# A 64-image chain of four convolution and scan layers on one core: the last norm's scale spread by a matmul in setup, and another order of the opening's convolution jobs

## The chip, the cores and the metric

The kernel runs on one NeuronCore of a Trainium2 chip. The metric is the device time in microseconds (us) from start to end of one launch; lower is better. Several launches are timed and the median is taken; one further launch is recorded by the hardware profiler. The engines are called PE (TensorE), DVE (VectorE), ACT (ScalarE), POOL (GpSimd) and SP (SyncE, which here only issues transfers).

## The reference, cut to what matters

The input is 64 images of 96 channels, 28 x 28, float32. Each passes through four layers, each with its residual:

- Layer 0: 1x1 expansion from 96 to 576 channels, norm, SiLU; a depthwise 5x5 convolution whose kernel is mixed per image from four experts; norm, SiLU; squeeze-and-excite; a 1x1 projection to 96 channels whose weights are also mixed from four experts; the last norm (`bn3`); add the input.
- Layers 1 and 3: expansion, norm, ReLU; depthwise 3x3, norm, ReLU; projection, the last norm, add the input.
- Layer 2: the image is cut in four quarters. On each: group norm, two 1x1 projections, a depthwise 3x3, and a selective scan (16 states, four directions), then group norm, a gate and a channel attention.

The last norm is `y * (g / sqrt(v + eps)) + ...` per output channel, so its factor can be multiplied into the projection's weights once, before any image:

```
inv = gamma * rsqrt(var + eps)
return (x - mean) * inv + beta
```

## The kernel before, in words

**Setup** (`Kernel.setup`, before L555) loads the weights in packed blobs, turns every norm into a scale and a bias (`bn`, L522, with `rsqrt`, L515: an add on DVE, then a power of -1/2 on POOL), multiplies `bn3`'s scale into the projection weights (`fold_bn3`, L535), expands the depthwise taps of layers 1 and 3 to diagonal blocks (`spread_taps`, L544, on POOL) and stores them and the four scaled experts of layer 0 to DRAM (`taps`, `w3_0`). Output channels lie along the free axis of the projection weights, so `fold_bn3` needs the scale as a row that is the same on all 128 lanes. Before the change this row is computed on all lanes: `bn3gr` and `bn3vr` are packed as 128 equal rows of 96, and the power runs over 128 x 96. That happens once for each of the four experts and once each for layers 1 and 3. Setup's scratch tiles come from a pool `fold` (two buffers per name) that is released when setup ends; the work tiles of the main part reuse its memory.

**The main part** keeps four images in flight. A *job* is one convolution layer on one image: `expand` (ten matmuls into PSUM, ACT applies norm and activation into padded tiles `border` and `hborder`, ACT's queue stores them to DRAM scratch `ex`), then per *unit* of channels `load` (SP loads shifted rows `rep`, and taps `wd`, from DRAM; for layer 0 POOL builds `wd` from the mixed kernel `kern`) and `depthwise` (20 matmuls a unit in layer 0, 12 a half-unit in layers 1 and 3, ACT evicts to `acc`), then `project` (18 or 10 matmuls, DVE adds to the image). Layer 0 has 9 units, layers 1 and 3 have 5 each; layer 0 also has `routing` and, ahead of its projection, `squeeze_excite`, which mixes the stored experts to `wp`. A `job(layer, t, ex)` names its layer, its image and its scratch.

Layer 2 on an image is two *halves*. `head` does norms, projections and the step sizes `dd`; `scans` then runs 12 groups of three DVE instructions per half (a product `b`, a scan `h`, a reversed scan `g`; before L1307, L1312, L1317), POOL combines them to `yc` (L1267), PE sums into `y` (L1241), and `tail` ends the half (last instruction L1396).

A *slot* runs layer 2 on image t beside the jobs of layer 1 on t+1, layer 0 on t+2 and layer 3 on t-1. There are 64 slots: slot 0 after an *opening*, 7 loop iterations of 8, then 7. The opening brings image 0 through layers 0 and 1 and image 1 through layer 0, and expands layer 1 of image 1 ahead.

The order on each engine is set by `Plan`: every operation has a due time, buffers and an estimated cost; `run` places operations greedily and chains each engine's instructions in that order, not earlier than 45 units before due. Buffers of one pool are taken in the order in which the operations were created (save `ps` and `gs`), so the order in which the jobs are written down also binds `rep` (3 buffers), `wd` (3) and `expert` (3). The hardware then runs each engine's list in order, waiting on semaphores only. Opening and slot 0 are one such plan, each loop iteration another; at the seam each engine goes on as soon as its own list is done.

Of the kernel before, what the change touches and what calls it, by code (L numbers as in the profile page):

```python
# [9 lines left out]
F32 = mybir.dt.float32  # L10
AF = mybir.ActivationFunctionType
ALU = mybir.AluOpType
AX = mybir.AxisListType
PSUM = bass.MemoryType.PSUM

P = 128
C = 96
# [4 lines left out]
E = 4  # L22
RH = 24
NS = 16
R = 6
# [6 lines left out]
NG = 9  # L32
# [42 lines left out]
def _rows(v):  # L75
    return np.tile(np.asarray(v)[None, :], (P, 1))
# [39 lines left out]
def pack_l0(ins):  # L116
    q = {k[len("L0_conv_") :]: np.asarray(v) for k, v in ins.items() if k.startswith("L0_conv_")}
    p = Pack()
    p.add("r_w1", q["r_w1"].T)
    p.add("r_b1", q["r_b1"][:, None])  # L120
    p.add("r_w2", q["r_w2"].T)
    p.add("r_b2", _rows(q["r_b2"]))
    p.add("w1", q["exp_w"].T)
    _pack_bn(p, "bn1", q, "bn1_g", "bn1_b", "bn1_m", "bn1_v", _lanes)
    _pack_bn(p, "bn2", q, "bn2_g", "bn2_b", "bn2_m", "bn2_v", lambda a: _groups(a, 16))

    dw = np.zeros((96 + RH, E, 360), np.float32)
    for e in range(E):
        dw[:96, e] = _taps(q["dw_w"][e].reshape(HID, 5, 5), 16).reshape(96, 360)
    dw.reshape(96 + RH, E * 360)[96:, : NG * P] = _groups(q["se_w2"], 16).transpose(2, 1, 0).reshape(RH, NG * P)  # L130
    p.add("dw", dw)
    p.add("mask", _pairs(np.repeat(np.eye(16, dtype=np.float32), 6, axis=0), 16))
    p.add("parity", _parity(16))
    p.add("se_w1", _groups(q["se_w1"].T, 16))
    b1 = np.zeros((96 + RH, 1), np.float32)
    b1[96:, 0] = q["se_b1"]
    p.add("se_b1", b1)
    p.add("se_b2", _groups(q["se_b2"], 16))
    p.add("bn3gr", _rows(q["bn3_g"]), once=True)
    p.add("bn3vr", _rows(q["bn3_v"]), once=True)  # L140
    _pack_bn(p, "bn3", q, "bn3_g", "bn3_b", "bn3_m", "bn3_v", None)
    return p

# [7 lines left out]
def pack_l1(ins, layer):  # L151
    pre = f"L{layer}_conv_"
    q = {k[len(pre) :]: np.asarray(v) for k, v in ins.items() if k.startswith(pre)}
    p = Pack()
    p.add("w1", q["w1"][:, :, 0, 0].T)
    _pack_bn(p, "bn1", q, "g1", "b1", "m1", "v1", _lanes)
    p.add("dw", _taps(q["wd"].reshape(HID, 3, 3), 32).reshape(P, 18 * 6), once=True)
    p.add("mask", _pairs(np.repeat(np.eye(32, dtype=np.float32), 4, axis=0), 32), once=True)
    _pack_bn(p, "bn2", q, "g2", "b2", "m2", "v2", _lanes)
    p.add("w3", _lanes(q["w3"][:, :, 0, 0].T))  # L160
    p.add("bn3gr", _rows(q["g3"]), once=True)
    p.add("bn3vr", _rows(q["v3"]), once=True)
    _pack_bn(p, "bn3", q, "g3", "b3", "m3", "v3", None)
    return p

# [280 lines left out]
class Kernel:  # L446
# [8 lines left out]
        g=(3, [P, 4, LSEQ]),  # L455
        yc=(3, [P, 4, SEQ]),
        B=(2, [P, 2, HALF]),
        C=(2, [P, 2, HALF]),
        dd=(4, [P, 3, HALF]),
        tmp=(2, [C, HALF]),  # L460
        gs=(3, [C, 32]),
        expert=(3, [P, 5 * C]),
# [7 lines left out]
        ps=(5, [P, 512]),  # L470
# [3 lines left out]
    def __init__(self, ctx, tc, x, out, blobs, packs):  # L474
        self.tc, self.nc = tc, tc.nc
        nc = tc.nc
# [12 lines left out]
        with self.tc.tile_pool(name="fold", bufs=2) as fold:  # L489
            engines = (nc.sync, nc.scalar, nc.sync, nc.scalar)  # L490
            self.c = []
            for i, (blob, p) in enumerate(zip(blobs, packs)):
                keep = self.tile([P, p.keep], f"blob{i}")
                once = fold.tile([P, blob.shape[1] - p.keep], F32, name=f"once{i}", bufs=1)
                engines[i].dma_start(keep, blob[:, : p.keep])
                engines[i].dma_start(once, blob[:, p.keep :])
                self.c.append(Consts(keep, once, p.at))
            self.setup(fold)
        self.slots = {name: n for name, (n, _) in self.POOLS.items()}
        work, psum = pool("work", 1), pool("psum", 1, space=PSUM)  # L500
        self.pools = {name: psum if name in ("ps", "y") else work for name in self.POOLS}
# [30 lines left out]
        nc.vector.tensor_tensor(bias, b, bias, ALU.subtract)  # L532
        return scale, bias

    def fold_bn3(self, c, w3, eps):  # L535

        nc = self.nc
        inv, tmp = self.inv
        self.rsqrt(inv, c("bn3vr"), eps, tmp)
        nc.vector.tensor_tensor(inv, inv, c("bn3gr"), ALU.mult)  # L540
        k = w3.shape[1]
        nc.vector.tensor_tensor(w3, w3, inv.rearrange("p (a o) -> p a o", a=1).to_broadcast([P, k, C]), ALU.mult)

    def spread_taps(self, out, taps, mask):  # L544

# [6 lines left out]
            ALU.mult,  # L552
        )

    def setup(self, fold):  # L555
        nc = self.nc
        c0, c1, c2, c3 = self.c
        self.eps, self.half1 = self.tile([C, 1], "eps"), self.tile([C, 1], "half1")
        nc.vector.memset(self.eps, 1e-5)
        nc.vector.memset(self.half1, 0.5)  # L560
        self.mhalf = self.tile([P, C], "mhalf")
        nc.vector.memset(self.mhalf, -0.5)

        self.inv = tuple(fold.tile([P, C], F32, name=f"inv{i}", bufs=1) for i in range(2))

        self.bn1_0 = self.bn(c0, "bn1", 1e-3, "l0")
        self.bn2_0 = self.bn(c0, "bn2", 1e-3, "l0")
        _, self.b3_0 = self.bn(c0, "bn3", 1e-3, "l0")
        for e in range(E):
            t = fold.tile([P, NG, C], F32, name="expert")  # L570
            nc.sync.dma_start(t.rearrange("p g o -> p (g o)"), self.experts[e])
            self.fold_bn3(c0, t, 1e-3)
            nc.sync.dma_start(self.w3_0[e], t.rearrange("p g o -> p (g o)"))

        self.ir = {}
        for layer, c in ((1, c1), (3, c3)):
            k = f"l{layer}"
            bn1 = self.bn(c, "bn1", 1e-5, k)
            bn2 = self.bn(c, "bn2", 1e-5, k)
            _, b3 = self.bn(c, "bn3", 1e-5, k)  # L580
            self.fold_bn3(c, c("w3"), 1e-5)
            self.ir[layer] = dict(c=c, bn1=bn1, bn2=bn2, b3=b3)

            for u in range(5):
# [5 lines left out]
                nc.sync.dma_start(self.taps[layer][u][:, : 32 * n], t[:, : 32 * n])  # L590


        with self.tc.tile_pool(name="fold_ps", bufs=1, space=PSUM) as banks:

            self.wdelta = self.tile([C + 1, C], "wdelta")
            ps = banks.tile([P, 512], F32, name="fold_ps0")
            nc.tensor.matmul(ps[:C, :C], c2("xdt"), c2("wdt")[:R], start=True, stop=True)
            nc.vector.tensor_copy(self.wdelta[:C], ps[:C, :C])
            nc.vector.tensor_copy(self.wdelta[C:], c2("wdt")[C:])
            ps = banks.tile([P, 512], F32, name="fold_ps")  # L600
            nc.tensor.matmul(ps[:C, :1], c2("p1"), c2("ln_b"), start=True, stop=True)
            nc.vector.tensor_tensor(c2("p1_b"), c2("p1_b"), ps[:C, :1], ALU.add)
            ps = banks.tile([P, 512], F32, name="fold_ps2")
            nc.tensor.matmul(ps[C : C + 1, :C], c2("ln_b"), c2("p2")[:C], start=True, stop=True)
            nc.vector.tensor_tensor(c2("p2")[C:], c2("p2")[C:], ps[C : C + 1, :C], ALU.add)
            for name in ("p1", "p2"):
                nc.vector.tensor_scalar(c2(name)[:C], c2(name)[:C], c2("ln_g"), None, ALU.mult)
        self.A = self.tile([P, NQ * J], "A")
        nc.scalar.activation(self.A, c2("A"), AF.Exp)
        nc.vector.tensor_scalar(self.A, self.A, -1.0, None, ALU.mult)  # L610
# [28 lines left out]
        self.ex = {(i, k): self.dpool.tile([HID, 2, 16, 32], F32, name=f"ex{i}_{k}") for i in range(3) for k in (3, 5)}  # L639
        for t in self.ex.values():  # L640
            nc.sync.dma_start(t[4 * P :].rearrange("c o r w -> c (o r w)"), self.pads[0][:64].rearrange("c o r w -> c (o r w)"))
        self.npad = self.ndecay = 0


# [781 lines left out]
            self.tail(q)  # L1426
        yield

    def slot(self, i, t, load, store, expanded=True, last=0):

        nc, pl, base, span = self.nc, self.plan, i * self.T, self.T
        keys = lambda t: [("x", t % 4, h) for h in range(2)]
        m = self.mamba(t, base, span, last < 2)
        next(m)
        jobs = []
        if last < 2:
# [16 lines left out]
        for _ in m:  # L1455
            pass

    def block(self):
        self.plan = Plan(self)
        return self.plan  # L1460
# [3 lines left out]
def mk_conv_seq_kernel(ctx, tc, x, out, blobs, packs):  # L1464
# [1 line left out]
    n = k.x.shape[0]  # L1466
    at = lambda v, i: v[bass.ds(i, 1)].rearrange("n c l -> (n c) l")
    pl = k.block()
    k.convs(
        -150.0, 150.0, [(k.job(0, 0, 1), None), (k.job(0, 1, 2), None), (k.job(1, 0, 1), None)], ahead=k.job(1, 1, 0)  # L1470
    )
    pl.due = -20.0
    k.head(k.half(0, 0))
    k.slot(0, 0, None, None)
    pl.run(-150.0)
    with tc.For_i(0, (n - 4) // 8, 1) as it:  # L1476
        pl = k.block()
# [34 lines left out]
```

## Time and profile before

| what | us |
|---|---|
| runs timed | 10371.73, 10323.82, 10363.91 |
| median | 10363.91 |
| the profiled execution's own time | 10374.65 |
| its span | 10372.8 |
| first routing instruction of the opening (L894) starts | 142.45 |
| first scan product (L1307) of slot 0 starts | 368.17 |
| last gate of slot 0 (L1396) starts | 524.84 |
| first scan product of the loop's first slot starts | 539.68 |

In the profile a line number L is that of the kernel's source; "x6" counts instructions; "idle before <- X" is time an engine had nothing to run, and X is what ended it. A float32 matmul shows as two records, so a layer-0 unit is 40 records of L786. "PEclk" is the share of full TensorE clock that was granted. Over the whole span PE is busy 9300.0 us (90%), DVE 8658.4 (83%), POOL 7409.3 (71%), ACT 6556.1 (63%), but these are averages over stages with different limits; setup, opening and slot 0 are 540 us of 10373.

### The profile page before, as it was taken

To read this page: it belongs to the slowest core of one execution; us is meant where nothing else is said; L and a number is where in the kernel's file an instruction comes from. 1 tells how busy PE (TensorE), PEld (TensorE's weight loads), DVE (VectorE), ACT (ScalarE), POOL (GpSimd) and SP (SyncE) were. 2 spreads that over 40 slices of the span, in tenths; PEclk is the share of its full clock that TensorE was granted. 3 is DMA by queue.
4 is the path that set the end of the run, shared out by engine and by line. 5 is a ranking of instruction groups with operands and counts; after the bars stand their busy time and mean duration, and the time that the engine had idled before them with its cause. 6 is when DMAs were issued, how large, how long until landed. Compare 5 with 4: busy or idle time off the path is not lost. (4 is left out here: it accounts for less than half of the span.)

```text
span 10372.8 us, 197146 instructions
## 1 busy us (share of the span) xinstructions
PE 9300.0 (90%) x75526; PEld 3900.2 (38%) x75526; DVE 8658.4 (83%) x8711; ACT 6556.1 (63%) x10733; POOL 7409.3 (71%) x7523
## 2 busy tenths in 40 slices
PE   4789998899989999899998999989999899998995
PEld 1333333334333433334333333333333333333342
DVE  1588897889878888788897899878897898888897
ACT  1466666666666666666665666666766666766663
POOL 5477776777767777677776777767776777767776
PEclk9889999999999999999999999989999999999997
DMA  4488887888878888788887888788887888877884
GB/s 140 136 225 222 233 239 214 222 226 238 235 213 220 225 235 231 201 225 226 231 240 204 224 240 235 214 218 220 228 242 211 223 231 219 230 218 212 231 237 114
DMA packets 1132620, 2262.68 MB, mean 218 GB/s; under 512 B 105984, under 2 KB 891136, under 8 KB 1131520
## 3 DMA queue, kind: packets, MB, share of 16 engines
q1 hardware_dynamic: 877120, 1750.78, 65.4%
q10 hardware_dynamic: 254528, 498.91, 13.7%
q8 instruction: 613, 10.04, 0.4%
q14 instruction: 359, 2.94, 0.1%
HBM read 1725.77 MB, written 523.50 MB: 217 GB/s over the span
## 5 line engine op out<-in xcount | busy, mean ns | idle before, releaser
L786 PE MATMUL ps<-rep,wd 128*32 128x392 f32 (+1 forms) x50688 | 4860.3, 522 | 383.5 <-DMA rep<-ex 93.9
L1312 DVE TENSOR_TENSOR_SCAN h<-decay,b 128x788 f32<-128x788 f32 x1536 | 2751.4, 1791 | 386.3 <-POOL g L1267 151.9
L786 PEld LDWEIGHTS ps<-rep,wd 128*32 128x32 f32 (+1 forms) x50688 | 1657.2, 112 | 3056.9 <-issue 2415.4
L1317 DVE TENSOR_TENSOR_SCAN g<-decay,b 128x788 f32<-128x788 f32 x1536 | 2727.4, 1776 | 28.8 <-DVE b L1307 3.2
L1267 POOL TENSOR_TENSOR yc<-h,g 128x392 f32<-128x392 f32 x1536 | 1576.1, 1045 | 1120.6 <-DVE b L1307 654.5
L797 ACT ACTIVATE acc<-ps,l_bn2b,l_bn2s 128x392 f32<-128x392 f32 x1728 | 1158.0, 674 | 1736.7 <-PE ps L786 1443.4
L1267 POOL TENSOR_TENSOR yc<-yc,C 128x392 f32<-128x392 f32 x1536 | 1565.0, 1037 | 456.8 <-DVE b L1307 385.3
L1307 DVE TENSOR_TENSOR b<-dd,B 128x784 f32<-128x784 f32 x1536 | 1816.3, 1182 | 43.1 <-issue 2.5
L1289 ACT ACTIVATE decay<-dd,A 128x784 f32<-128x784 f32 x1536 | 1364.3, 942 | 718.1 <-DMA dd<-ddd 422.6
L1267 POOL TENSOR_TENSOR g<-h,g 128x392 f32<-128x392 f32 x1536 | 1558.7, 1035 | 309.6 <-DVE b L1307 297.6
L1267 POOL TENSOR_TENSOR yc<-yc,g 128x392 f32<-128x392 f32 x1536 | 1433.6, 952 | 145.7 <-DVE b L1307 145.7
L684 PE MATMUL ps<-x,blob 96*128 96x392 f32 x3072 | 1296.7, 558 | 121.6 <-PEq L1476 33.6
L668 ACT ACTIVATE border<-ps,l_bn1b,l_bn1s 128x392 f32<-128x392 f32 x1536 | 986.8, 675 | 395.1 <-PE ps L684 277.3
L548 POOL TENSOR_TENSOR wd<-kern,blob 96x640 f32<-96x640 f32 x576 | 765.4, 1335 | 301.8 <-PE ps L786 173.7
L684 PEld LDWEIGHTS ps<-x,blob 96*128 96x128 f32 x3072 | 581.2, 206 | 780.1 <-issue 286.2
L855 PE MATMUL ps<-acc,blob 128*96 128x392 f32 (+1 forms) x2560 | 826.9, 505 | 29.2 <-ACT acc L797 13.0
L855 PE MATMUL ps<-acc,wp 128*96 128x392 f32 x2304 | 781.1, 497 | 34.7 <-DVE wp L995 34.3
L1289 ACT ACT_TABLE_LOAD x422 | 541.4, 1283 | 73.0 <-ACT border L668 37.5
L855 PEld LDWEIGHTS ps<-acc,wp 128*96 128x96 f32 x2304 | 371.6, 164 | 437.8 <-issue 380.9
L1241 PE MATMUL y<-yc,blob 128*32 128x392 f32 x3072 | 450.6, 524 | 86.7 <-POOL yc L1267 86.6
L855 PEld LDWEIGHTS ps<-acc,blob 128*96 128x96 f32 (+1 forms) x2560 | 352.7, 162 | 461.7 <-issue 361.7
L1082 POOL TENSOR_TENSOR gs<-gs,mhalf 96x2 f32<-96x2 f32 x256 | 188.7, 737 | 449.0 <-ACT gs L1079 273.9
(145 smaller groups left out, 7448.9 us busy)
## 6 DMA issues: line engine op xcount, KB each, us to landing
rep<-ex SPq DMA_DIRECT2D x1024, 448.0 KB, 7.5
rep<-ex SPq DMA_DIRECT2D x1984, 224.0 KB, 5.1
ex<-border ACTq DMA_DIRECT2D x512, 480.0 KB, 5.7
dd<-ddd SPq DMA_DIRECT2D x384, 588.0 KB, 6.8
wd<-taps SPq DMA_DIRECT2D x512, 384.0 KB, 6.7
ex<-border ACTq DMA_DIRECT2D x256, 512.0 KB, 5.6
B<-bcd SPq DMA_DIRECT2D x256, 392.0 KB, 4.1
C<-bcd SPq DMA_DIRECT2D x256, 392.0 KB, 5.2
```

The lines of the kernel that those rows point to most:

```text
L548: self.nc.gpsimd.tensor_tensor(out, taps.rearrange("k (n a) -> k n a", a=1).to_broadcast([k, n, cb]), mask.rearrange("k (a c) -> k a c", a ...
L668: nc.scalar.activation(dst, ps()[:, :HALF].rearrange("p (r o w) -> p o r w", o=2, w=28), d["func"], bias=bias[:, t : t + 1], scale=scale[: ...
L684: nc.tensor.matmul(ps()[:, :HALF], w1[:, t * P : t * P + P], x[:, h * HALF : (h + 1) * HALF], start=True, stop=True)
L786: nc.tensor.matmul(ps()[lo : lo + 32, :HALF], w, rep()[: (k + 1) * cb, b, :, 2 - off + dx : 30 - off + dx], start=(dx == 0), stop=(dx == k ...
L797: nc.scalar.activation(acc()[lo : lo + n], ps()[lo : lo + n, :HALF], d["func"], bias=bias[lo : lo + n, at : at + 1], scale=scale[lo : lo + ...
L855: nc.tensor.matmul(banks[o]()[:C, :HALF], w, a, start=(i == 0), stop=(i == (8 if d["layer"] == 0 else 4)))
L1241: nc.tensor.matmul(y()[32 * j : 32 * j + 32, :HALF], c("sel"), ys[j]()[:, 2 * u : 2 * u + 2], start=(k == 0 and u == 0), stop=(k == 1 and ...
L1267: nc.gpsimd.tensor_tensor(*vs, op)
L1289: nc.scalar.activation(fs[:, :, u, :, :SEQ], d()[:, :2].rearrange("p o (i l) -> p o i l", i=2), AF.Exp, scale=self.A[:, at : at + 1],)
L1307: nc.vector.tensor_tensor(out, v, w, ALU.mult)
L1312: lambda h=h, ff=ff: nc.vector.tensor_tensor_scan(flat(h()), ff, b, 0.0, ALU.mult, ALU.add),
L1317: lambda g=g, ff=ff: nc.vector.tensor_tensor_scan(flat(g())[:, ::-1], ff[:, ::-1], b[:, ::-1], 0.0, ALU.mult, ALU.add),
```

## The change

Two things are changed; loop and final slots keep, instruction for instruction, the order they had on every engine.

Setup: `bn` already makes `bn3`'s scale as a column (one channel per lane, 96 x 1). `row_of` multiplies an identity matrix by this column on DVE and multiplies a matrix of ones by the result on PE, which gives the row on all 128 lanes in PSUM; `fold_bn3` reads it from there. The row is made once for layer 0 and once each for layers 1 and 3. The packed rows `bn3gr` and `bn3vr` go, an identity `eye` comes, and `mhalf` shrinks from 96 columns to 9. The four experts get four buffers and are all loaded early; their scaling on DVE and their stores move to setup's end. The PSUM pool `fold_ps` now spans all of setup.

Opening: `opening` replaces a call of `convs` and writes down the jobs in another order, and slot 0's layer 2 gets due times 45 units earlier (`lead`).

```diff
-    p.add("bn3gr", _rows(q["bn3_g"]), once=True)
-    p.add("bn3vr", _rows(q["bn3_v"]), once=True)
+    p.add("eye", np.eye(C, dtype=np.float32), once=True)
...
-    def fold_bn3(self, c, w3, eps):
+    def row_of(self, banks, scale, eye, name):
         nc = self.nc
-        inv, tmp = self.inv
-        self.rsqrt(inv, c("bn3vr"), eps, tmp)
-        nc.vector.tensor_tensor(inv, inv, c("bn3gr"), ALU.mult)
+        nc.vector.tensor_scalar(eye[1], eye[0], scale, None, ALU.mult)
+        ps = banks.tile([P, 512], F32, name=name)
+        nc.tensor.matmul(ps[:, :C], self.ones[:C], eye[1], start=True, stop=True)
+        return ps[:, :C]
+
+    def fold_bn3(self, row, w3):
         k = w3.shape[1]
-        nc.vector.tensor_tensor(w3, w3, inv.rearrange("p (a o) -> p a o", a=1).to_broadcast([P, k, C]), ALU.mult)
+        self.nc.vector.tensor_tensor(w3, w3, row.rearrange("p (a o) -> p a o", a=1).to_broadcast([P, k, C]), ALU.mult)
...
-        self.mhalf = self.tile([P, C], "mhalf")
+        self.mhalf = self.tile([P, NG], "mhalf")
...
-        _, self.b3_0 = self.bn(c0, "bn3", 1e-3, "l0")
-        for e in range(E):
-            t = fold.tile([P, NG, C], F32, name="expert")
+        s3, self.b3_0 = self.bn(c0, "bn3", 1e-3, "l0")
+        eye = c0("eye"), fold.tile([C, C], F32, name="diagonal", bufs=2)
+        row = self.row_of(banks, s3, eye, "fold_row0")
+        experts = [fold.tile([P, NG, C], F32, name="expert", bufs=E) for e in range(E)]
+        for e, t in enumerate(experts):
             nc.sync.dma_start(t.rearrange("p g o -> p (g o)"), self.experts[e])
-            self.fold_bn3(c0, t, 1e-3)
-            nc.sync.dma_start(self.w3_0[e], t.rearrange("p g o -> p (g o)"))
...
-            _, b3 = self.bn(c, "bn3", 1e-5, k)
-            self.fold_bn3(c, c("w3"), 1e-5)
+            s3, b3 = self.bn(c, "bn3", 1e-5, k)
+            self.fold_bn3(self.row_of(banks, s3, eye, f"fold_row{layer}"), c("w3"))
...
+        for e, t in enumerate(experts):
+            self.fold_bn3(row, t)
+            nc.sync.dma_start(self.w3_0[e], t.rearrange("p g o -> p (g o)"))
         self.npad = self.ndecay = 0
...
-        m = self.mamba(t, base, span, last < 2)
+        m = self.mamba(t, base - lead, span, last < 2)
...
+    def opening(self):
+        pl = self.plan
+        first, second, other, ahead = self.job(0, 0, 1), self.job(1, 0, 1), self.job(0, 1, 2), self.job(1, 1, 0)
...
+        def units(d, us, due, each):
+            for i, u in enumerate(us):
+                pl.due = due + each * i - 14.0
+                self.load(d, u)
+                pl.due = due + each * i
+                self.depthwise(d, u)
...
+        expand(first, -150.0)
+        self.routing(first)
+        units(first, range(4), -150.0, 5.0)
+        expand(other, -140.0)
+        self.routing(other)
+        units(first, range(4, NG), -130.0, 5.0)
+        project(first, -105.0)
+        units(other, range(5), -103.0, 5.0)
+        expand(second, -85.0)
+        units(second, range(5), -68.0, 4.0)
+        project(second, -48.0)
+        pl.due = -46.0
+        self.head(self.half(0, 0))
+        units(other, range(5, NG), -44.0, 5.0)
+        project(other, -24.0)
+        expand(ahead, -18.0)
...
-    k.convs(
-        -150.0, 150.0, [(k.job(0, 0, 1), None), (k.job(0, 1, 2), None), (k.job(1, 0, 1), None)], ahead=k.job(1, 1, 0)
-    )
-    pl.due = -20.0
-    k.head(k.half(0, 0))
-    k.slot(0, 0, None, None)
+    k.opening()
+    k.slot(0, 0, None, None, lead=45.0)
     pl.run(-150.0)
```

## The prediction

> **What bounds it now.** The page's 90% PE is an average; the change touches only the first 540 us. So I first read busy time by stretch (columns: stretch, length, busy us of PE, PE's weight load, DVE, ACT and POOL, granted TensorE clock, DMA share, GB/s):
>
> ```profile
> 0.00:50.00 50.00, 5.46 (x14) 2.35 (x14) 13.67 (x53) 3.46 (x4) 38.43 (x23) 1.00 0.41 135
> 50.00:100.00 50.00, 0.48 (x1) 0.00 (x0) 7.37 (x11) 0.00 (x0) 47.60 (x7) 1.00 0.16 55
> 100.00:150.00 50.00, 5.12 (x12) 2.46 (x13) 10.34 (x14) 2.21 (x5) 36.77 (x7) 1.00 0.30 92
> 150.00:200.00 50.00, 45.97 (x350) 19.00 (x352) 7.11 (x23) 22.01 (x40) 13.06 (x10) 1.00 0.82 225
> ...
> 400.00:450.00 50.00, 9.93 (x26) 2.48 (x26) 48.52 (x36) 11.02 (x17) 39.93 (x44) 0.57 0.16 49
> ```
>
> Setup, to 142 us, is POOL alone. From 150 PE is full. In slot 0 DVE is full (48.52 of 50) and PE nearly empty. The groups of the first 150 us say what POOL does:
>
> ```profile
> L520 POOL TENSOR_TENSOR inv<-inv,mhalf 128x96 f32<-128x96 f32 x6 | 94.0, 15669 | 5.9 <-DVE expert L542 5.0 <-DVE blob L542 0.9
> L548 POOL TENSOR_TENSOR taps<-once 128x768 f32<-128x768 f32 x8 | 11.8, 1477 | 4.3 <-DMA once<-w_dram 4.3
> L540 DVE TENSOR_TENSOR inv<-inv,once 128x96 f32<-128x96 f32 x6 | 7.9, 1314 | 92.8 <-POOL inv L520 92.8
> ```
>
> Six powers of 15.67 us fill it, and DVE waits for them (92.8). The timeline shows what releases the opening, then DVE's way through slot 0:
>
> ```profile
> 142.45 2.72 DVE L894 TENSOR_REDUCE rw<-x 96x1 f32<-96x784 f32 x3 [3.83 <-DMA taps<-taps]
> ...
> 368.17 1.62 DVE L1307 TENSOR_TENSOR b<-dd,B 128x784 f32<-128x784 f32 x1 [2.16 <-DMA dd<-ddd]
> ...
> 494.76 1.77 DVE L1317 TENSOR_TENSOR_SCAN g<-decay,b 128x788 f32<-128x788 f32 x1
> ...
> 524.84 0.75 DVE L1396 SCALAR_TENSOR_TENSOR x<-ps,cz,x 96x196 f32<-96x196 f32 x2 [4.80 <-ACT cz L1390]
> ...
> 539.68 0.97 DVE L1307 TENSOR_TENSOR b<-dd,B 128x784 f32<-128x784 f32 x1
> ```
>
> L894 waits for setup's last transfers, since its tile takes over the memory of `fold`. Layer 2 of image 0 runs 368.17 to 496.5; the loop's first product follows at 539.68. That last mark is my yardstick: the rest of the program has the same order before and after, so its 9833 us (10372.8 - 539.7) should stay.
>
> **What the Trainium skill says.** *GPSIMD Engine Reference*, section 3.1, gives a two-input operation some 2.6 cycles an element; the trace's power is far dearer, 0.545 us on 96x1 and 15.67 on 128x96, 0.16 us a column, so the trace decides. [...]the trace has 2.4 at the median. *TensorE: Matmul & The Clock Gate*, Part 1, says that an idle array falls to half clock; the trace agrees, with 0.50 granted from 420 to 440 where PE is busy 4.28 of 20 us.
>
> **Part 1, the row.** Removed: 6 x 15.67 = 94.0 us of POOL, plus six L540 and L519 on DVE. Added, three times: a DVE product of 96x96 (the like of L607, 0.27), a matmul (L597, 0.63 for its two records) and the clearing of `ones` (0.14 for 128x96). These 3 us lie beside POOL, which still works through its taps; without that cover they would cost their 3 us. The product with the experts reads PSUM now; 1.05 became at most 1.3 by the like of L885, beside POOL too.
>
> What is late next? POOL keeps 27 us of work. Small powers start at 16.06; layer 0's take 3.45, layers 1 and 3 take 2.8 each, one tap 1.47, the clearing of borders 2.25: POOL stands at 28.8 with two of ten taps built. The other eight share two buffers, and each third build waits until a store has landed: 1.48 + 2.4 = 3.9 us a pair, 15.6 for four pairs, so 44.5. On SP six halo stores of 256 KB stand between the taps' stores; I add 1. SP then issues the four expert stores, moved behind the taps: 1.77 MB at 300 GB/s (early slices of the transfer rows reach 301 to 394) is 5.9, plus 2 for landing: 54 to 55. The built order has the opening's first reduce (L899 after) wait for these stores. Their data is ready: the loads go out at 12 to 13 us and land in 5.5 at the median, DVE's four products are done by some 34. So setup ends near **55 instead of 142.45: -87**. Bounds: 48 if stores don't hinder each other (-94); 68 if a tap's store takes 5 us, as a busy DMA did with `rep<-ex` (5.1) (-74).
>
> At the opening's start ACT waited 3.6 us for halo stores (L668 <- DMA ex<-border). They are issued before the expert stores now: **-3** (0 to -4).
>
> **Part 2, the opening,** in times of before. PE's stretch of first and second image read:
>
> ```profile
> 230.14 12.09 PE L855 MATMUL ps<-acc,wp 128*96 128x392 f32 x36
> 242.16 3.56 PE L786 MATMUL ps<-rep,wd 96*32 96x392 f32 x40
> ...
> 266.51 10.26 PE L786 MATMUL ps<-rep,wd 128*32 128x392 f32 x96 [0.89 <-DMA wd<-taps]
> ```
>
> A layer-0 unit is 3.4 us, a layer-1 half-unit 2.2, a layer-0 projection 12.1, an expansion 6.65. In the new order PE does 14 units, not 15, before the first projection: image 0 is ready at 239. Expansion to 246. Now nothing covers its way through DRAM: `rep` buffers go in the order written, so the other image's last four units queue behind. First store issued near 241.5, landing 5.7, the first `rep` (448 KB) 7.5 more: PE restarts near 255, **9 us idle**. Nine half-units (19.8), the projection (6.5), eviction and add end at 283, where before image 0 was ready at 325.4. From there to the first scan product took 42.8 (325.4 to 368.17). The chain is the same; ACT has fewer evictions but a gate's table load (1.28) in it. I take 327 for 368.17: scans start **41 earlier**.
>
> Is that kept? Twenty-four groups at 4.8 us (405.89 to 439.64 is seven) and some 12 of other DVE work end at 454; before they ended at 496.5. But PE, DVE and ACT have not finished their lists. By the built order POOL makes four of the nine `wd` of slot 0's layer-0 job only after its last `yc`, PE therefore has four units after the last `y`, then squeeze-and-excite, then projection, and DVE has the expert mixing and both image adds *behind* layer 2's last gate and ahead of the loop. Working it out: last `y` at 462, four units 14 to 23 (474.68 shows 5.7 for one at low clock), gate and sums near 480 to 485, mixing 15 (483.77 to 498.75 before, its expert loads one by one), rest of the projection 9, second add at 510. Expansion 6.7, then the loop's own 14.6 to its routing result (L1396 524.84 to L912 539.1): first product of the loop at 532 to 533. **So of 41 only 7 stay.** Before, this job ran beside the scans. Bounds: +12 if mixing waits for its loads longer (the opening's took 35 from sums to add, 207 to 242), -41 if PE's clock stays full and the tail hides.
>
> SP's list: `dd` loads stand behind four expert loads that need mixing; by my times they are issued five us before `dd` is stored, cost nothing, and would push the scans by what they are late.
>
> **Sum:** -87 - 3 - 7 = **-97 us**. Against the profiled execution, 10374.65 (span plus 1.85), that is 10278. That execution lay 10.7 above the median 10363.91; against the median it is **10267**. The runs shown spread 48 us.
>
> **The rivals.**
> *The whole lead arrives.* PE's idle 40 of 50 us in slot 0 speaks for it, POOL's order of `wd` against it. -87 - 3 - 41: 10233.
> *The tail costs more than the lead brings*, by 12 to 20 us: 10364 - 90 + 15 = 10289; for it, the 35 us from sums to add; against it, fewer transfers then (103 GB/s at 480 to 500).
> *Setup is held by transfers, so the power's removal brings only half.* 14.09 MB move before 150 us; at the 135 GB/s of the first 50 us they would need 104. Then setup gains 38, and the sum is -48: 10316. Against it: those slices with work reach 300.
> *Slower, by place of tiles.* `mhalf` shrinks from 384 to 36 bytes a lane, and every later constant and work tile lies 320 bytes lower. Should that slow DVE, POOL or the transfers, it does so in 63 slots of 156.1 us (9833 / 63). From 97 / 63 = 1.54 us a slot, 1%, the gain is gone; 2.4 us a slot makes 10418. Nothing in the trace shows a dependence on place; nothing excludes it.
>
> **The numbers.** About 0.5%, 52 us, is what a measurement of this kernel can tell from no change: faster means below 10312. The forecast 0.60, the whole lead 0.17, costly tail 0.13, held setup 0.07, slower 0.03. The first three are faster: 0.90; the fourth same, 0.07. The range reaches from the whole lead with setup at its fast bound (-94 - 4 - 41: 10225) and 5 us below it for the spread of runs, 10220, to the costly tail by 20 with setup at its slow bound and nothing at the opening's start (-74 + 20: 10310), 10312 with the same thought rounded to the edge of no change.
>
> **What would show it.** Right: no POOL instruction over 2 us before 60; L899 near 55, released by an expert store; PE idle some 9 us ahead of layer 1's first units; the first scan product 131 earlier (near 237), the loop's first only 97 earlier (near 443), with L872 ahead of it. Wrong: L899 after 75, the loop's first product before 415 or after 470, or a span from there to the end other than 9833 by over 25.

## The result, and the profile after

The changed kernel takes **10250.44 us**, the median of four runs (10225.01 to 10259.11), against 10360.36 for the kernel before in the same series: a ratio of 0.9896, 95% interval 0.9866 to 0.9926. In a second series of its own (experiment e4) it is 0.9883, 0.9865 to 0.9902. The forecast was 10267: the direction was right, and the median is 17 us below the forecast. The profiled execution took 10225.01 us, its span is 10223.2: the fastest of its four, which matters below.

I read the same views as for the kernel before. First, busy time by stretch (stretch, length, busy us of PE, PE's weight load, DVE, ACT, POOL, granted TensorE clock, DMA share, GB/s), of the kernel after:

```profile
0.00:50.00 50.00, 8.10 (x20) 3.88 (x20) 22.96 (x63) 3.46 (x4) 28.93 (x29) 1.00 0.78 261
50.00:100.00 50.00, 43.28 (x280) 17.99 (x284) 9.81 (x28) 22.55 (x40) 10.42 (x8) 0.90 0.70 213
...
150.00:200.00 50.00, 38.38 (x356) 15.27 (x358) 3.56 (x11) 11.68 (x24) 5.25 (x4) 0.93 0.82 192
...
300.00:350.00 50.00, 33.49 (x225) 11.85 (x225) 48.93 (x42) 25.39 (x44) 43.00 (x45) 0.68 0.18 47
350.00:400.00 50.00, 35.66 (x304) 15.74 (x305) 20.68 (x30) 10.42 (x31) 26.60 (x27) 0.80 0.31 81
```

PE is full from 50 us on, not from 150: two stretches in which POOL worked alone are gone. At 300 to 350 DVE is full and POOL is busy for 43 of 50 (slot 0's scans). In the stretch after it DVE falls to 20.68 of 50 and POOL to 26.60, while PE has 35.66: that is the tail which the prediction described. (The clock column needs care: the trace's clock records begin at 172 us in the kernel before and at 66 in this one, and the column shows 1.00 where there is no record. The 1.00 of setup, with PE nearly idle, is therefore no reading of the clock.) The groups of the first 150 us say where POOL's time went:

```profile
L550 POOL TENSOR_TENSOR taps<-once 128x768 f32<-128x768 f32 x8 | 11.8, 1474 | 5.6 <-DMA once<-w_dram 3.4 <-DMA taps<-taps 1.1 <-issue 1.0
...
L518 POOL TENSOR_TENSOR l_bn1s<-l_bn1b,mhalf 128x5 f32<-128x5 f32 x3 | 3.6, 1186 | 5.1 <-DVE l_bn3b L517 5.1
...
L518 POOL TENSOR_TENSOR l_bn3s<-l_bn3b,mhalf 96x1 f32<-96x1 f32 x3 | 1.6, 546 | 0.0
```

The group of six powers at 15669 ns is gone; only the small powers and the taps stay, each as dear as before. Of those six, four computed the same row, that of layer 0, once for each expert. Computing it once, with nothing else changed, would have removed three powers, 47 of the 94 us (an estimate, 3 x 15.67); no run has that edit alone. The other half, by the same estimate, is what the matmul removes. DVE's timeline holds the marks of the prediction (L899, L1312, L1322 and L1401 are L894, L1307, L1317 and L1396 of before):

```profile
50.77 2.72 DVE L899 TENSOR_REDUCE rw<-x 96x1 f32<-96x784 f32 x3 [11.94 <-DMA w<-expert]
...
233.56 1.67 DVE L1312 TENSOR_TENSOR b<-dd,B 128x784 f32<-128x784 f32 x1
...
361.45 1.77 DVE L1322 TENSOR_TENSOR_SCAN g<-decay,b 128x788 f32<-128x788 f32 x1
...
390.27 0.75 DVE L1401 SCALAR_TENSOR_TENSOR x<-ps,cz,x 96x196 f32<-96x196 f32 x2 [4.80 <-ACT cz L1395]
...
410.51 0.62 DVE L872 SCALAR_TENSOR_TENSOR x<-ps,l_bn3b,x 96x392 f32<-96x392 f32 x1 [5.30 <-PE ps L860]
...
436.80 0.17 DVE L917 TENSOR_TENSOR ps<-ps,blob 128x4 f32<-128x4 f32 x1 [23.67 <-PE ps L912]
...
437.34 0.97 DVE L1312 TENSOR_TENSOR b<-dd,B 128x784 f32<-128x784 f32 x1
```

Setup ends 91.7 us earlier (142.45 to 50.77), slot 0's scans start 134.6 earlier (368.17 to 233.56), but the loop starts only 102.3 earlier (539.68 to 437.34). The image add L872 stands between gate and loop, as predicted. Two stretches of the same kernel tell what goes on in setup's last 25 us, first with engines at work and few transfers, then the reverse:

```profile
25.00:30.00 5.00, 0.74 (x2) 0.50 (x2) 4.94 (x5) 0.00 (x0) 5.00 (x6) 1.00 0.30 75
...
45.00:50.00 5.00, 0.00 (x0) 0.00 (x0) 0.00 (x0) 0.00 (x0) 0.00 (x0) 1.00 0.92 358
```

From 45 to 50 no engine works at all; transfers run at 358 GB/s. The page's idle ahead of L899 agrees: 11.94 us, ended by an expert store.

### The profile page after: what moved, and what is told of

Read it like the earlier page. It is cut to its first block, busy times and chain, and to the rows that moved or that the text cites. A ratio compares the mean times of both kernels' runs of the same rounds, so it can differ in the third digit from the quotient of the medians.

```text
span 10223.2 us, 197108 instructions
## 1 busy us (share of the span) xinstructions
PE 9274.7 (91%) x75532; PEld 3896.7 (38%) x75532; DVE 8661.9 (85%) x8703; ACT 6554.9 (64%) x10733; POOL 7313.9 (72%) x7517
## 5 line engine op out<-in xcount | busy, mean ns | idle before, releaser
L1317 DVE TENSOR_TENSOR_SCAN h<-decay,b 128x788 f32<-128x788 f32 x1536 | 2751.4, 1791 | 363.8 <-POOL g L1272 130.3
L1322 DVE TENSOR_TENSOR_SCAN g<-decay,b 128x788 f32<-128x788 f32 x1536 | 2727.4, 1776 | 28.0 <-ACT decay L1294 2.5
L1272 POOL TENSOR_TENSOR yc<-h,g 128x392 f32<-128x392 f32 x1536 | 1574.3, 1044 | 1095.7 <-DVE b L1312 660.8
L1272 POOL TENSOR_TENSOR yc<-yc,C 128x392 f32<-128x392 f32 x1536 | 1559.5, 1033 | 443.8 <-DVE b L1312 376.0
L1312 DVE TENSOR_TENSOR b<-dd,B 128x784 f32<-128x784 f32 x1536 | 1826.0, 1189 | 43.3 <-issue 4.0
L1272 POOL TENSOR_TENSOR g<-h,g 128x392 f32<-128x392 f32 x1536 | 1560.6, 1036 | 326.3 <-DVE b L1312 302.8
L1272 POOL TENSOR_TENSOR yc<-yc,g 128x392 f32<-128x392 f32 x1536 | 1434.3, 952 | 153.4 <-DVE b L1312 153.4
L860 PE MATMUL ps<-acc,blob 128*96 128x392 f32 (+1 forms) x2560 | 826.8, 505 | 29.1 <-ACT border L673 14.7
L890 DVE SCALAR_TENSOR_TENSOR ps<-expert,rw,ps 128x480 f32<-128x480 f32 (+1 forms) x384 | 255.5, 665 | 226.9 <-DMA expert<-w 185.2
```

Source lines behind the costliest of these rows:

```text
L860: nc.tensor.matmul(banks[o]()[:C, :HALF], w, a, start=(i == 0), stop=(i == (8 if d["layer"] == 0 else 4)))
L1272: nc.gpsimd.tensor_tensor(*vs, op)
L1312: nc.vector.tensor_tensor(out, v, w, ALU.mult)
L1317: lambda h=h, ff=ff: nc.vector.tensor_tensor_scan(flat(h()), ff, b, 0.0, ALU.mult, ALU.add),
L1322: lambda g=g, ff=ff: nc.vector.tensor_tensor_scan(flat(g())[:, ::-1], ff[:, ::-1], b[:, ::-1], 0.0, ALU.mult, ALU.add),
```

## The experiments

All kernels below carry the same work unless the text says otherwise. The marks come from one profile of each kernel: the first reduce (setup's end), the first scan product of slot 0, the first of the loop, and what is left from there to the span's end ("rest").

| kernel | first reduce | slot 0 | loop | rest | clock | ratio to before, 95% |
|---|---|---|---|---|---|---|
| before | 142.45 | 368.17 | 539.68 | 9833.1 | 0.938 | |
| e0, before again | 141.74 | 366.91 | 539.89 | 9826.3 | 0.939 | 0.9995 [0.998, 1.001] |
| e11, before, tiles 320 B lower | 141.85 | 368.88 | 542.13 | 9840.5 | 0.936 | 0.999 [0.9978, 1.0002] |
| e2, new order alone | 141.80 | 325.76 | 530.29 | 9793.3 | 0.941 | 0.998 [0.9968, 0.9993] |
| e1, new setup alone | 50.67 | 271.46 | 444.03 | 9824.6 | 0.936 | 0.989 [0.9863, 0.9918] |
| after | 50.77 | 233.56 | 437.34 | 9785.9 | 0.941 | 0.9896 [0.9866, 0.9926] |
| e4, after again | 51.68 | 233.97 | 441.44 | 9795.8 | 0.938 | 0.9883 [0.9865, 0.9902] |
| e3, after, tiles at old places | 51.61 | 238.92 | 441.04 | 9824.0 | 0.934 | 0.9913 [0.9887, 0.994] |
| e5, slot 0's jobs due 30 earlier | 51.31 | 231.40 | 429.26 | 9820.2 | 0.939 | 0.9883 [0.9863, 0.9903] |
| e6, lead 0 | 51.18 | 236.65 | 429.29 | 9823.3 | 0.936 | 0.9891 [0.9874, 0.9907] |
| e9, lead 20 | 51.01 | 235.48 | 430.68 | 9845.5 | 0.937 | one run |
| e7, experts first | 55.02 | 237.99 | 441.46 | 9788.5 | 0.941 | 0.9867 [0.985, 0.9883] |
| e8, expert stores on ACT's queue | 54.81 | 234.40 | 439.03 | 9823.8 | 0.938 | one run |
| e10, lead 0 and ten taps buffers | 51.30 | 233.50 | 426.14 | 9818.3 | 0.936 | 0.9881 [0.9855, 0.9907] |

The marks repeat to about 1 us at the first reduce and to 4 at the loop (after and e4). The rest does not: 9785.9 to 9845.5, in kernels whose loop has the same order of instructions.

### e0: the kernel before once more

The edit is none.

> The kernel before, unchanged, run again with a profile of its own, to learn how long its loop takes in another execution. Theory A (the loop's pace varies from execution to execution, the change doesn't touch it): first product of the loop again at 538 to 541 us, since setup and opening wait on a fixed chain; from there to the end anything from 9785 to 9835 us. Theory B (the lower place of the tiles makes the loop faster): from the loop's first product to the end 9825 to 9840 us again, because this kernel has the old places. Ratio to the kernel before 1.000 within 0.002 under both.

The rest was 9826.3, which both theories allowed, so this profile doesn't choose between them. The 35 runs of before in this series, each with its own mean clock, show more: 10411.7 us on average at a clock of 0.933 (3 runs), 10376.8 at 0.937 (10), 10353.3 at 0.940 (3), 10326.06 at 0.942 (1). That is 8.0 us for 0.001 of clock, with a correlation of -0.89. Time and clock go together, and the runs of this one kernel spread over 94 us (10326.06 to 10420.3). Which of the two leads is not shown: the granted clock was 0.50 where PE idled (420 to 440 us of the kernel before), so a loop that is slow for another reason could lower the mean too.

### e1: the new setup alone

```diff
-    k.opening()
-    k.slot(0, 0, None, None, lead=45.0)
+    k.convs(
+        -150.0, 150.0, [(k.job(0, 0, 1), None), (k.job(0, 1, 2), None), (k.job(1, 0, 1), None)], ahead=k.job(1, 1, 0)
+    )
+    pl.due = -20.0
+    k.head(k.half(0, 0))
+    k.slot(0, 0, None, None)
```

> The new setup with the opening of before (its convolution order, and layer 2 of slot 0 without its lead of 45). Theory A (the parts add, setup brings nearly all): the opening's first reduce at 50 to 52 us, first scan product of slot 0 at 276 to 279 (91 to 92 earlier than before), first product of the loop at 446 to 450, so 90 to 93 us faster at that mark, and a ratio near 0.991. Rival (the new order is what carries the gain into the loop, because without it the opening gives some of setup's gain back in a new wait): loop's first product after 460, ratio above 0.9935. Theory B (place of tiles speeds up the loop): a further 47 us, ratio near 0.987.

Loop at 444.03: 95.7 of the 102.3 us come from setup alone, 91.8 by its end and 3.9 more in the opening. My theory A had the first scan product at 276 to 279 and the loop at 446 to 450; they came at 271.46 and 444.03, somewhat earlier still. ACT's wait of 3.6 us for a halo store (`border` <- DMA `ex<-border`) is not among its waits here, as the prediction's second term had it. The time, 111.6 below before's median, is more than the mark; on that see e11.

### e2: the new order alone

The setup is that of before; opening and lead are those of the change.

> The setup of before with the new opening and its lead of 45. Theory A (of some 40 us by which the scans start earlier, the tail of slot 0's layer-0 job leaves 7 to 11): the opening's first reduce at 142 to 144 us, first scan product of slot 0 at 323 to 328, first product of the loop at 528 to 533, ratio near 0.999. Rival (the whole lead arrives in the loop): the loop's first product near 499, ratio near 0.996. Rival (the two changes share a gain, alone the order brings nothing or costs): loop's first product at 540 or later, ratio 1.000 or above. The tiles lie at the old places here, so theory B adds nothing.

Scans 42.4 earlier than in before (41 were predicted for this part), loop 9.4 earlier (7 were). So most of the scans' earlier start is lost here too, and the two parts of the change add: 95.7 + 9.4 = 105.1, against 102.3 in the profile of both together, 98.2 in the second.

### e4: the changed kernel once more

The edit is none.

> The changed kernel, unchanged, run again with a profile of its own, to learn how much of its first profile repeats. Theory A (setup and opening are fixed chains, the loop's pace goes with the granted TensorE clock of the execution): first reduce at 50 to 52 us, slot 0's first scan product at 233 to 239, first product of the loop at 437 to 441; from there to the end 9785 to 9795 where the mean clock is 0.941 again, 9810 to 9835 where it is 0.939 or less. Theory B (the change itself made the loop 47 us faster): 9785 to 9795 at any clock. Ratio to before 0.990 within 0.002 under A.

Setup and scans agree with the first profile within 1 us, the loop comes 4.1 later. Three of these arise in the first of the four layer-0 units behind the scans: PE takes 6.54 us for it at a granted clock of 0.52, where the first profile has 3.54 at 1.00. The rest was 9795.8 at a clock of 0.938, which theory A had not allowed for a clock below 0.941; the clock's mean explains the rest's length only roughly in a single profile.

### e3 and e11: the places of the tiles

e3 puts the changed kernel's tiles at the old places, e11 puts the tiles of before at the new ones:

```diff
e3, against the changed kernel
-        self.mhalf = self.tile([P, NG], "mhalf")
+        self.mhalf = self.tile([P, C], "mhalf")
e11, against the kernel before
-        nc.gpsimd.tensor_tensor(out, tmp, self.mhalf[: var.shape[0], :n], ALU.pow)
+        nc.gpsimd.tensor_tensor(out, tmp, self.mhalf_row[: var.shape[0], :n], ALU.pow)
...
-        self.mhalf = self.tile([P, C], "mhalf")
+        self.mhalf = self.tile([P, NG], "mhalf")
+        self.mhalf_row = fold.tile([P, C], F32, name="mhalf_row", bufs=1)
+        nc.vector.memset(self.mhalf_row, -0.5)
```

> The changed kernel with one edit: the constant mhalf is given its old size of 96 columns, so that every constant and work tile made after it lies where it lay before (320 bytes a lane higher than in the changed kernel). Theory A (places don't matter; the loop's pace varies from run to run): first product of the loop at 436 to 439 us, from there to the end within the scatter of the other profiles (9785 to 9835), ratio to before 0.990 within 0.002, the same as the changed kernel. Theory B (the lower places make the loop some 47 us faster): the loop takes 9825 to 9840, ratio near 0.994.

> The kernel before with one edit: mhalf is made with 9 columns, as in the changed kernel, and its 96-column version for setup's powers lies in setup's own pool, so that all later constants and work tiles lie 320 bytes a lane lower, as in the changed kernel; nothing else changes. It is for what is left over: in the runs so far the times differ from before by 10 to 25 us more than the first product of the loop is earlier, and the changed kernel put back to the old places was 97 us below the mean of before where the changed kernel itself was 121 in another series. Theory A (the leftover is scatter of the loop's pace): ratio 1.000 within 0.0015, first product of the loop at 538 to 541. Theory B (the low places make the loop some 20 us faster): ratio 0.998 or lower. Rival of the prediction (the low places cost 1.5 us a slot): ratio 1.009.

e11 is 0.999, 0.9978 to 1.0002. A cost of 1.5 us a slot (1.009) is excluded: the prediction's slower rival falls. A small gain from the low places, up to some 23 us, is not excluded, and e3's ratio, which lies above that of e4 with overlapping intervals, doesn't exclude it either. But e2 had 9793.3 at the old places and e1, e5 and e6 had 9820 to 9825 at the new ones, so the 47 us by which the first profile of after has a shorter rest than before are not explained by the places. The loop's first product (441.04 in e3, 542.13 in e11) missed the ranges of my theories A by 2 and by 1.

### e5, e6, e9: what eats the lead

```diff
e5  in slot: -  self.convs(base, span, ...)   +  self.convs(base - early, span, ...)   with early=30 for slot 0
e6           -  k.slot(0, 0, None, None, lead=45.0)   +  k.slot(0, 0, None, None)
e9           -  k.slot(0, 0, None, None, lead=45.0)   +  k.slot(0, 0, None, None, lead=20.0)
```

> The changed kernel with one number more: the convolution jobs of slot 0 alone are due 30 us earlier in the planner's list, so that POOL makes their weights between layer 2's y rather than behind the last yc, and one of TensorE's layer-0 units is left after the last y where there were four. My theory (the tail of slot 0's layer-0 job behind layer 2 is what keeps most of the lead from arriving in the loop): first product of the loop near 407 to 420 us, 17 to 30 earlier than the changed kernel, ratio to before 0.986 to 0.989. Rival (the scans are slowed by what now lies between their steps, so that the last product comes later by as much as the tail shrinks): loop's first product at 434 to 441, ratio 0.990.

> The changed kernel with the lead of slot 0's layer 2 taken back from 45 to 0; the new opening's order is kept. By the built order layer 2's scans are then placed later among the opening's and slot 0's units, and all of slot 0's layer-0 units come ahead of its last y, as before the change. My theory (what the opening's order gains in image 0 stays lost behind the layer-0 job whichever way the two are interleaved): first scan product 5 to 20 us later than in the changed kernel, first product of the loop within 5 of its 437 to 441, ratio 0.990. Rival 1 (the lead is needed): loop's first product at 444 or later, no better than the new setup with the old opening. Rival 2 (the lead is too long and makes the tail): loop's first product before 432.

> The changed kernel with a lead of 20 for slot 0's layer 2, where the change has 45 and the kernel without a lead reached the loop's first product at 429.3, 8 to 12 us before the changed kernel. Marks decide, one profile. Theory (with 45 the layer-0 job ends after the scans, with 0 the scans after the layer-0 units and the gate behind them; both ends meet in between): loop's first product at 420 to 428. Rival (both kernels at 429.3 are held by one chain that the lead doesn't move: layer-0 weights on POOL, the last units, mixing, projection at low clock): 427 to 432. A third way (the planner's list is what decides, and 20 falls on the side of 45): 434 to 441.

In the changed kernel POOL's timeline behind the scans is the mechanism that the prediction had named:

```profile
370.43 1.97 POOL L1272 TENSOR_TENSOR yc<-yc,C 128x392 f32<-128x392 f32 x2
372.37 3.86 POOL L550 TENSOR_TENSOR wd<-kern,blob 96x640 f32<-96x640 f32 x3
377.45 1.31 POOL L550 TENSOR_TENSOR wd<-kern,blob 96x640 f32<-96x640 f32 x1 [1.22 <-PE ps L791]
```

and PE's timeline shows what follows from it, four units and then the projection:

```profile
356.83 6.56 PE L791 MATMUL ps<-rep,wd 96*32 96x392 f32 x40 [7.19 <-POOL wd L550]
...
373.73 3.54 PE L791 MATMUL ps<-rep,wd 96*32 96x392 f32 x40 [0.42 <-POOL wd L550]
...
377.46 3.54 PE L791 MATMUL ps<-rep,wd 96*32 96x392 f32 x40
...
381.36 6.91 PE L791 MATMUL ps<-rep,wd 96*32 96x392 f32 x80
...
396.21 14.25 PE L860 MATMUL ps<-acc,wp 128*96 128x392 f32 x36 [1.66 <-DVE wp L1000]
```

The last `yc` is ready at 372.4; four of nine `wd` are built only then. With the jobs due 30 earlier (e5), PE has one unit left behind the last `y`, and the loop starts at 429.26, 8 to 12 us before after and e4: the tail does cost part of what the earlier start brought. The 17 to 30 that I expected are not there. From the last `yc` to the second image add the changed kernel takes 38.1 us and e5 27.2, three units less; the rest of that stretch (one unit, sums, mixing, projection) stays. And the last `yc` comes 2.5 us later, at 374.9, probably since the `wd` now stand between the scans' instructions on POOL. In e6, without a lead, the roles are exchanged: the units come before the last `y`, and wait. First PE:

```profile
368.11 5.31 PE L791 MATMUL ps<-rep,wd 96*32 96x392 f32 x40 [9.35 <-POOL wd L550]
```

then on DVE:

```profile
402.52 0.62 DVE L872 SCALAR_TENSOR_TENSOR x<-ps,l_bn3b,x 96x392 f32<-96x392 f32 x1 [5.60 <-PE ps L860]
403.39 0.75 DVE L1401 SCALAR_TENSOR_TENSOR x<-ps,cz,x 96x196 f32<-96x196 f32 x2 [0.25 <-ACT cz L1395]
...
429.29 0.97 DVE L1312 TENSOR_TENSOR b<-dd,B 128x784 f32<-128x784 f32 x1
```

The last unit waited 9.35 us for its `wd`, which stands in POOL's list among the products of L1272; gate and image add end together at 403. So a lead of 45 is worse at the loop's first product than a lead of 0 (e6 429.29, e9 with 20 430.68), though it brings the last scan 11 us forward (361.45 against 372.74). Against e1, which has the old order and no lead, the new order without the lead brings 14.7 us, and the lead takes 8 to 12 of it back. My own expectation for e6, within 5 of 437 to 441, was wrong, and so was the first scan product (3 us later than in after, where I had 5 to 20); its second rival was right. For e9 too the rival was right (427 to 432), and my 420 to 428 wrong; that is one profile. In all three kernels the second image add comes at 402 to 404 and the loop some 27 us later, as it does in after: that last piece, an expansion and the routing behind it, doesn't move with the order.

### e7, e8, e10: what ends setup now

```diff
e7      for e, t in enumerate(experts):
            nc.sync.dma_start(t.rearrange("p g o -> p (g o)"), self.experts[e])
     +  for e, t in enumerate(experts):
     +      self.fold_bn3(row, t)
     +      nc.sync.dma_start(self.w3_0[e], t.rearrange("p g o -> p (g o)"))
     ...  (the same three lines go from setup's end)
e8   -  nc.sync.dma_start(self.w3_0[e], ...)     +  nc.scalar.dma_start(self.w3_0[e], ...)
e10  -  t = fold.tile([P, 768], F32, name="taps")   +  t = fold.tile([P, 768], F32, name="taps", bufs=10)
     -  k.slot(0, 0, None, None, lead=45.0)      +  k.slot(0, 0, None, None, lead=0.0)
```

> The changed kernel with the products of the four expert tiles with the row, and their stores, put back right behind their loads, ahead of the taps; the row by matmul and all else is kept. My theory (setup now ends with what SP has queued behind the last tap: four expert stores whose data lie ready for long cost some 8 to 10 us at the end): first reduce at 43 to 48 us where the changed kernel has 50.8, and all later marks earlier by the same. Rival (SP stands waiting at the expert stores while taps are ready, so that the taps' stores and with them POOL's eight later builds slip): first reduce at 51 or later. Ratio to before 0.989 to 0.990 or 0.990 to 0.991: too near to each other for the times, the marks decide.

> The changed kernel with the four expert stores issued from ACT's DMA queue instead of SP's; they stand at the same place in the program. Marks decide, one profile. My theory (setup ends late because the expert stores stand behind the last tap's store on SP, though their data lie ready near 39 us): they are issued near 39 us, the first reduce comes at 45 to 48, and every later mark is 3 to 6 us earlier: slot 0's first scan product at 228 to 231, the loop's first at 432 to 438. Rival (transfers are the limit: 13 MB in 52 us, and the slices of the stretch are busy up to 400 GB/s): first reduce at 50 or later as in the changed kernel.

> The changed kernel with two edits that don't touch each other: slot 0's layer 2 without its lead (first product of the loop at 429.3 in the run without a lead), and ten buffers for the taps of setup instead of two, so that POOL builds its ten taps without waiting for a store. The first reduce tells of the second edit alone. Theory 1 (POOL's and the stores' turns with two buffers still set the end of setup, as the prediction had it; 4.0 us of POOL's waits in the changed kernel): first reduce at 46 to 48.5, first product of the loop at 424 to 428. Theory 2 (the transfers as a whole set it: two kernels in which the expert stores came earlier ended setup at 54.8 and 55.0, later than the changed kernel, because the taps' stores slipped): first reduce at 50 us or later, first product of the loop at 428 to 433. Ratio to before 0.988 within 0.002 in both cases.

e7 ends setup at 55.02, later than the changed kernel. Its waits of SP (total, times, longest) say why:

```profile
SPq L579 <- DVE expert L544: 14.6, 3, 12.7
SPq L596 <- POOL taps L550: 10.6, 8, 2.6
```

My theory (43 to 48) was wrong and the rival right: SP stands 14.6 us at the expert stores until DVE has made the products, and the stores of finished taps stand behind. So POOL's third build is late:

```profile
37.49 2.91 POOL L550 TENSOR_TENSOR taps<-once 128x768 f32<-128x768 f32 x2 [9.80 <-DMA taps<-taps]
```

e8 was to free SP, and did not. Its waits of SP have a row that the other kernels don't have,

```profile
SPq L643 <- DMA w<-expert: 8.2, 1, 8.2
```

a halo store on SP that waits 8.2 us for an expert store on ACT's queue. In the trace both raise the same semaphore: the expert store landed at 38.77, and SP issued the halo store at 38.78. POOL waits 10.41 us for taps in turn, and setup ends at 54.81, where the rival (50 or later) had it, but for another cause. e8 thus says nothing on the rate of the transfers.

e10 removed the turns of POOL and stores that the prediction had priced at 15.6 us. POOL's timeline, then SP's, then DVE's:

```profile
28.84 6.57 POOL L550 TENSOR_TENSOR taps<-once 128x768 f32<-128x768 f32 x5
35.35 1.84 POOL L640 MEMSET border<- 128x1024 f32 x2
```

```profile
22.42 13.33 SPq L593 DMA_DIRECT2D taps<-taps  x9
36.33 5.63 SPq L643 DMA_DIRECT2D ex<-border  x6
42.05 5.05 SPq L646 DMA_DIRECT2D w<-expert  x4
```

```profile
51.30 2.72 DVE L899 TENSOR_REDUCE rw<-x 96x1 f32<-96x784 f32 x3 [8.92 <-DMA w<-expert]
```

POOL is done with the taps at 35.4 instead of 42.0 and setup still ends at 51.30. But the edit moved more than the turns. In the changed kernel POOL clears the borders at 25.2, ahead of its third tap, and the six halo stores go out between the taps' stores; the expert stores follow the last tap:

```profile
26.18 0.54 SPq L643 DMA_DIRECT2D ex<-border  x1
...
36.70 0.45 SPq L643 DMA_DIRECT2D ex<-border  x1
...
42.92 4.05 SPq L646 DMA_DIRECT2D w<-expert  x4
```

In e10 the clearing stands behind all taps (35.35), and with it all six halo stores. So six halo stores (256 KB each) and four expert stores (432 KB), 3.3 MB, are issued between 36 and 47 and landed near 51. What e10 shows is that freeing POOL of its turns, in this order, brings nothing; an edit that frees the turns and keeps the halo stores early was not run. That the transfers' rate sets the last 15 us fits e10: from 35 to 50 the DMA engines are busy for 82, 99 and 94% of each 5 us. No run took bytes away, so this is argued, not shown. The loop of e10 starts at 426.14, where theory 1 had it though theory 2 was right on the first reduce. That is 3.2 us before e6, the other kernel without a lead, which is within what a mark scatters, and 11 to 15 before the changed kernel; in time (0.9881) it can't be told from it (0.9883).

## Why the prediction was right, step by step

- **Setup, -87.** Measured -91.7, -90.8 in e4. The six powers were the bound, and the added product, matmul and clearing lie beside POOL. No POOL instruction before 60 exceeds 2 us. The chain behind them ran much as told: POOL's last eight builds, which share two buffers and wait for stores of 384 KB (2.4 us at the median), took from 27.4 to 42.0, 14.5 us where 15.6 were estimated; SP issued the expert stores from 42.9, and they release L899. All in all setup ended 4 us before the estimate. What the prediction did not have is that this chain is not alone: in e10 the turns are gone and setup ends no earlier, with the transfers busy in their place. That the chain gave nearly the right size is therefore in part luck. The rival "held by transfers" was half right: transfers do fill the end of setup, but at 253 to 358 GB/s and not at the 135 it was built on.
- **The opening's start, -3.** Without the new order (e1) the loop is 3.9 nearer to the first reduce than in before (in e0, 0.9 farther), and ACT's wait for the halo store is gone.
- **The scans 41 earlier.** e2: 42.4. The pause of PE ahead of layer 1's units, predicted at 9 us, is there in PE's timeline of the kernel after:

```profile
158.10 10.04 PE L791 MATMUL ps<-rep,wd 128*32 128x392 f32 x96 [6.64 <-DMA rep<-ex]
169.90 4.26 PE L791 MATMUL ps<-rep,wd 128*32 128x392 f32 x48 [1.76 <-DMA rep<-ex]
175.93 2.26 PE L791 MATMUL ps<-rep,wd 128*32 128x392 f32 x24 [1.77 <-DMA rep<-ex]
179.65 2.57 PE L791 MATMUL ps<-rep,wd 128*32 128x392 f32 x28 [1.46 <-DMA wd<-taps]
```

  in four pieces, 6.64 + 1.76 + 1.77 + 1.46 = 11.6. The rows and taps of each unit come one after the other, not all with the first.
- **Of the 41 only 7 stay.** e2: 9.4 stay. The tail was told in the right order: the last four `wd` behind the last `yc`, four units, sums, mixing, projection, second add, expansion, routing. Its dates, shifted by setup's 92: sums 388 to 393 (389.5 measured), second add 418 (410.5), loop 440 to 441 (437.34 and 441.44). The second add is where the estimate was 8 us too dear: PE ran the four units in 3.5 us each, the cheap end of my 14 to 23 us, and the mixing took 9.3 us (L890 from 391.23 to L1000 at 400.48), not 15. Expansion and routing gave 5 of it back: 26.8 where I had 21.3. With setup as measured, the rival "the whole lead arrives" would have had the loop near 405, the costly tail near 460; neither happened.
- **The rest stays 9833.** Here the first profile overstepped my mark: 9785.9, 47 less, where 25 was the limit. The step that failed is the reading of one profiled rest as a constant. Runs of before alone span 94 us, together with the granted clock; the first profile of after was the fastest of four runs, at 0.941. Over all fourteen profiles the rest runs from 9785.9 to 9845.5, and both ends belong to the new setup and order. Nor is it the seam that passes something on: the loop's first slot takes 142.5 to 143.7 us in all fourteen. The differences gather over the loop's seven iterations, which take from 1233 us (clock 0.96, in e2) to 1270 (0.94, in e11). Not settled is a smaller part: in the series with several runs the mean time lies 2 to 39 us further below the mean of before than the loop's first product does, in most of them by 9 to 23. Some of this is scatter: e0, which is the kernel before itself, already lies 7 us further below; e3 lies 2 us less far. The places of the tiles don't explain it well, as e2 has 13 us of it at the old ones, though e11 leaves room for up to 23. A part may be real; no run decides it.

## What to carry to other kernels

A broadcast along lanes belongs on PE when the engine that would compute it in full is the one that sets the stage: 94 us of POOL went for a few us on DVE and PE, which were idle. (Half of it would have gone by computing a repeated row once.) Work that is started earlier gains only if every list it shares is shortened too: the new order started DVE's scans 42 us earlier, but POOL had the scans' products and the convolution's weights in one list, and whichever came second was late. And where the effect is 10 us in 10 ms, compare marks inside the trace, which repeated to 1 to 4 us, and not times, which spread by 94.

## What the runs showed of the hardware that was not expected

- The time of one kernel goes with the mean granted TensorE clock of the execution, 8.0 us for each 0.001 between 0.933 and 0.942, over 35 runs of the kernel before; which is the cause is open. In a single piece the effect is plain: one layer-0 unit took 3.54 us at a granted clock of 1.00 and 6.54 at 0.52 (after and e4).
- Two queues are not independent where the program hands one semaphore to transfers of both: 8.2 us of waiting on SP in e8, for moving four stores to an idle queue.
- In e10 the four expert stores took 5.2 us from issue to landing at the median, behind six halo stores; in e7, where no transfer had run for some 8 us before, the same stores took 2.5.
